# Four small edits to a fused attention and mixture-of-experts kernel: ones multiplied at the start, the sort's first step moved, the first gate later, the last bias earlier

## The chip, the core and the metric

The kernel runs on one core of a Trainium2 chip. The time is the device's, in microseconds (us), from launch to end; lower is better. The engines are TensorE (PE in the profile), VectorE (DVE), ScalarE (ACT), GpSimd (POOL) and SyncE, which here issues most transfers (SP). Each takes its instructions in its own order and waits for the others through semaphores.

## The reference

The input is `x`, 64 sequences of 64 tokens with 256 features, and one type (0, 1 or 2) for each sequence. Everything is fp32. Two blocks follow each other, each with a residual:

```python
x = x + attention(cond(x, type))
x = x + moe(cond2(x, type))
```

- `cond`: a gated FFN (`gelu(x @ wi0) * (x @ wi1) @ wo`, 256 to 1024 to 256) with the weights of the sequence's type, and one with shared weights. A gate mixes the two: a softmax over two logits, from the first token of each sequence, `softmax(relu(concat(expert[:, 0], share[:, 0]) @ g0) @ g1)`.
- `attention`: causal, 16 heads of 16, within each sequence, with biases.
- `cond2`: two typed experts and three shared FFNs, mixed by a gate in the same manner.
- `moe`: a router of three layers, the two best of eight experts for each token, at most 10 tokens per sequence and expert, and for each expert `relu(x @ W1 + b1) @ W2 + b2`, scaled by the router's weight and added up.

## The kernel before, in words

The sequences are sorted by type, so that most groups share weights. The sort runs on the chip: `sort()` is a Python generator which yields between its steps, so that a few small operations at a time can be put between others. Its first step (lines 577 and 579) turns the types into 64 x 3 flags on DVE; two empty steps later a pair of small products with a matrix of ones counts each type and ranks each sequence (tile `p`). The ones are filled by POOL in `masks()` (line 501).

Sequences are handled in eight superblocks of eight (512 tokens). A layer multiplies with Strassen's scheme: seven products p1 to p7 of half-size blocks, whose sums are made on DVE, ACT and POOL. In the up products (`strassen`) each product needs a PSUM bank of a pool of four, until DVE or ACT has read it; p3 is added into the bank of p5, and so must wait until DVE has taken p5 out of it (line 256). The down products go into accumulating banks of their own, `sa...` (p1, p6, p2, p7) and `sb...` (p5, p3, p4). `layer` gives each superblock items of a `first` (up) and a `second` (down) half, and `pipeline` runs the `first` of the next item before the `second` of this one.

At the start, `load_x(0)` fetches the tokens of superblock 0 in two halves, eight pieces of the shared weights follow on the same queue, and the types come by ACT's queue (line 444). `turn_x(0)` transposes the tokens on TensorE into two banks (tile `px`), of which ACT copies the first and DVE the second (line 835). `tc.issue_after` holds DVE's copy behind the last cast of the counters (`K.cast`). Then come the sums for the products, on DVE and POOL, and the Strassen products of the shared layer (names ending in `c`).

Side work is slipped in through a list, `between`: each call of `tick` takes one entry, and where an entry is flagged as needing room, ticks that offer none pass it by. An entry of `None` is an empty step. The sort is trickled in this way (15 entries), and in the typed layers (names ending in `e`) so are the gate and the attention of an earlier superblock: `begin_cond(s)` appends the gate's steps and then `attention(s)`. It is called after the `first` of one item and before the `second` of the one before it. The gate's steps are

- `hidden`: products of the typed tokens (`tw1`) and the shared part with `g0` (tile `pha`), copied by ACT (line 1248),
- `add_up`, `logits`, `spread`: small products (`pfa`, `plga`, `pgwa`) with a softmax between them,
- `sums`: the weighted sum on DVE, after which `fetch1` of the next superblock issues its eight fetches on SP.

`m2`, `m3` and `whole` are the last attention steps of the superblock before; for superblock 0 they are empty. In a typed superblock there are 12 ticks in each of two `first` halves and 3 in the `second` of item 0, after p1/p6, p2/p7 and p5/p3. `tw1` is filled by `fetch_typed`: the typed result is written to DRAM (`spillt`) and read back in sorted order, in eight transfers, each with an address read from a table.

In the last stage, `down` multiplies the hidden values of an expert with its second weights for five tiles of 128 slots (`po`). For each tile DVE adds the bias, ACT scales by the router's weight, and POOL scatters the rows with an add into the output. For the very last tile the bias is scaled first, by ACT (line 2023), so that one DVE operation (line 2024) does the rest. This scaled bias lies in one of the four slots that the results go round in: the one of tile 1.

Which instruction stands where on its engine is settled when the program is built: the framework's scheduler goes by the order of the code and by what it reckons to be ready, so that neighbours can change places (p4 runs ahead of p3 in the first superblock).

## Time and profile before

| | us |
|---|---|
| median of the runs | 2747.27 |
| the three runs | 2747.27, 2744.07, 2747.38 |
| the profiled execution, its own time | 2744.14 |
| its span (first to last instruction) | 2742.5 |
| busy in it: TensorE | 2709.1 |
| busy in it: VectorE | 1626.9 |
| busy in it: GpSimd | 1065.2 |
| busy in it: ScalarE | 837.1 |

The profile is of one execution; its times are counted from its first instruction. A row of the timeline gives the start, the length, the engine, the line, the operation, the tile written and read, the shape and the number of instructions; brackets at its end hold the time for which the engine had been idle, and what ended that. Most matmuls are recorded by a helper on line 119, so they are told apart by their tiles. An fp32 product stands as two records, a transpose as one. The lengths of matmuls overlap their successors, so starts are what counts. In the table by windows, the columns of an engine are its busy time and its number of instructions, and behind them comes the granted TensorE clock, as a share of the full one. In the span's first 12.84 us the clock isn't recorded and the table gives 1.00.

### The profile page before, as it was taken

To read this page: it belongs to the slowest core of one execution; us is meant where nothing else is said; L and a number is where in the kernel's file an instruction comes from. 1 tells how busy PE (TensorE), PEld (TensorE's weight loads), DVE (VectorE), ACT (ScalarE), POOL (GpSimd) and SP (SyncE) were. 2 spreads that over 40 slices of the span, in tenths; PEclk is the share of its full clock that TensorE was granted. 3 is DMA by queue.
4 is the path that set the end of the run, shared out by engine and by line. 5 is a ranking of instruction groups with operands and counts; after the bars stand their busy time and mean duration, and the time that the engine had idled before them with its cause. 6 is when DMAs were issued, how large, how long until landed. Compare 5 with 4: busy or idle time off the path is not lost.

```text
span 2742.5 us, 38338 instructions
## 1 busy us (share of the span) xinstructions
PE 2709.1 (99%) x13765; PEld 2232.6 (81%) x13765; DVE 1626.9 (59%) x2931; ACT 837.1 (31%) x1535; POOL 1065.2 (39%) x1121
## 2 busy tenths in 40 slices
PE   8999999999999999999999999999999999999998
PEld 7888887677767778888888888888888888877777
DVE  7887467888887774535546766667443333332443
ACT  2221124544444332212222222222222222322333
POOL 4555123343335667634323332325323322324332
PEclk9999999999999999999999999999999999999999
DMA  4554545343342123652443434444200000013330
GB/s 118 159 173 141 191 149 185 97 128 128 104 147 88 63 101 135 207 183 81 154 136 126 150 132 146 147 139 135 70 17 6 9 5 6 5 52 79 96 92 2
DMA packets 236365, 293.47 MB, mean 107 GB/s; under 512 B 141624, under 2 KB 199824, under 8 KB 236048
## 3 DMA queue, kind: packets, MB, share of 16 engines
q1 hardware_dynamic: 214608, 231.44, 26.9%
q0 software_dynamic: 21344, 58.54, 6.3%
q8 instruction: 109, 1.79, 0.3%
q10 hardware_dynamic: 224, 1.05, 0.1%
q14 instruction: 80, 0.66, 0.1%
HBM read 208.80 MB, written 83.99 MB: 107 GB/s over the span
## 4 chain that ended last, share of the span: by engine, by line
PE 91%; DVE 4%; issue 2%; DMA 2%; ACT 0%; SPq 0%; POOL 0%; POOLq 0%; DVEq 0%; ACTq 0%
PE sad L119 6%; PE p5r L119 5%; PE p1r L119 5%; PE po L119 5%; PE sbd L119 4%; PE sat L119 4%; PE p5d L119 3%; PE p1d L119 3%; PE sbt L119 3%; PE p6r L119 2%; PE p4r L119 2%; PE p7r L119 2%; PE p5e L119 2%; PE p1e L119 2%; PE p5t L119 2%; PE sac L119 2%
## 5 line engine op out<-in xcount | busy, mean ns | idle before, releaser
L198 POOL TENSOR_TENSOR arena<-arena 128x512 f32<-128x512 f32 (+1 forms) x175 | 236.3, 1350 | 667.2 <-DVE arena L195 659.3
L199 POOL TENSOR_TENSOR arena<-arena 128x512 f32<-128x512 f32 (+1 forms) x175 | 213.5, 1220 | 18.0 <-DVE arena L196 17.0
L119 PE MATMUL sad<-arena 128*128 128x256 f32 x768 | 176.7, 380 | 0.0
L119 PE MATMUL po<-arena 128*128 128x256 f32 (+1 forms) x704 | 169.8, 399 | 0.1
L119 PEld LDWEIGHTS sad<-arena 128*128 128x128 f32 x768 | 144.0, 190 | 19.6 <-issue 0.8
L119 PEld LDWEIGHTS po<-arena 128*128 128x128 f32 x704 | 132.9, 190 | 28.4 <-issue 11.0
L119 PE MATMUL p5r<-arena 128*128 128x256 f32 x640 | 149.7, 381 | 0.5 <-DVE arena L256 0.5
L119 PE MATMUL p1r<-arena 128*128 128x256 f32 x640 | 150.0, 382 | 0.0
L195 POOL TENSOR_TENSOR arena<-arena 128x256 f32<-128x256 f32 (+1 forms) x55 | 45.1, 821 | 260.8 <-ACT arena L1740 80.7
L1902 POOL DMA_INDIRECT xs<-arena,slot_i x64 | 62.6, 978 | 199.9 <-ACT arena L1898 108.7
L119 PEld LDWEIGHTS p1r<-arena 128*128 128x128 f32 x640 | 120.0, 190 | 21.2 <-issue 5.9
L119 PEld LDWEIGHTS p5r<-arena 128*128 128x128 f32 x640 | 120.8, 190 | 17.6 <-DVE arena L256 1.4
L119 PE MATMUL sbd<-arena 128*128 128x256 f32 x576 | 134.8, 381 | 0.0
L195 DVE TENSOR_TENSOR arena<-arena 128x512 f32<-128x512 f32 (+2 forms) x127 | 96.8, 762 | 63.2 <-ACT arena L332 34.2
L119 PEld LDWEIGHTS sbd<-arena 128*128 128x128 f32 x576 | 108.5, 190 | 17.5 <-POOL arena L199 2.2
L188 POOL TENSOR_TENSOR arena<-arena 128x256 f32<-128x256 f32 (+1 forms) x53 | 47.9, 905 | 184.8 <-DMA arena<-in_L_cond_share_wo 43.3
L119 PE MATMUL sat<-arena 128*128 128x256 f32 x512 | 118.6, 382 | 0.8 <-POOL arena L198 0.8
L196 DVE TENSOR_TENSOR arena<-arena 128x512 f32<-128x512 f32 (+2 forms) x127 | 108.8, 856 | 3.5
L2028 POOL DMA_INDIRECT out<-arena,rows_i x40 | 61.9, 1547 | 123.4 <-ACT arena L2027 66.9
L119 PEld LDWEIGHTS sat<-arena 128*128 128x128 f32 x512 | 96.2, 190 | 14.0 <-POOL arena L198 1.2
L332 ACT ACTIVATE arena<-arena 128x512 f32<-128x512 f32 x144 | 90.3, 628 | 45.6 <-DVE arena L267 21.6
L119 PE MATMUL p5d<-arena 128*128 128x256 f32 x384 | 99.7, 382 | 2.4 <-DVE arena L256 2.4
(452 smaller groups left out, 6243.5 us busy)
## 6 DMA issues: line engine op xcount, KB each, us to landing
arena<-sums_i SPq DMA_DIRECT2D x32, 896.0 KB
arena<-sums_2i SPq DMA_DIRECT2D x32, 896.0 KB
arena<-sums_2o SPq DMA_DIRECT2D x32, 896.0 KB
arena<-in_L_ffn_eW SPq DMA_DIRECT2D x16, 1024.0 KB
arena<-sums_o SPq DMA_DIRECT2D x16, 896.0 KB
spill<-arena SPq DMA_DIRECT2D x24, 512.0 KB
arena<-spill POOLq DMA_DIRECT2D x24, 512.0 KB, 6.1
sums_i<-arena POOLq DMA_DIRECT2D x12, 896.0 KB, 3.9
```

The costliest lines, as they stand in the source:

```text
L119: nc.tensor.matmul(o, lhsT=lhsT, rhs=rhs, start=start, stop=stop, skip_group_check=shared_bank)
L188: eng.tensor_add(s1, a21, a22)
L195: eng.tensor_sub(t1, b12, b11)
L196: r = eng.tensor_sub(t2, b22, t1)
L198: eng2.tensor_sub(t3, b22, b12)
L199: return r.ins, eng2.tensor_sub(t4, b21, t2).ins
L332: nc.scalar.activation(c_out(ij), src, AF.Relu)
L1902: nc.gpsimd.indirect_dma_start(out=to.rearrange("e n w -> (e n) w"), out_offset=bass.IndirectOffsetOnAxis(ap=slot_i[:, n, i : i + 1], axis=0),
L2028: nc.gpsimd.indirect_dma_start(out=out_rows, out_offset=bass.IndirectOffsetOnAxis(ap=row_i[:, u : u + 1], axis=0), in_=eo, in_offset=None, ...
```

## The change

It has four parts.

1. The matrix of ones is filled by DVE near the top, and TensorE multiplies it with itself six times into a bank `idle` that nothing reads. POOL's fill of it is gone.
2. The first step of the sort (the two DVE operations) is issued ahead of the tokens' transposes, and `K.cast`, behind which DVE's copy of the tokens stands, now is its second operation. A `yield` more keeps the later steps at the same entries of the list.
3. For superblock 0, two empty entries are put ahead of the gate's first step.
4. In the last expert, the scaled bias is made before the first tile's products, into a slot of its own.

```diff
@@ setup
     ident = const.tile([P, P], F32, name="ident")
     make_identity(nc, ident)
+    K.ones = const.tile([P, P], F32, name="ones")
+    nc.vector.memset(K.ones, 1.0)
+
+    idle = bank("idle")
+    for _ in range(6):
+        mm(idle[:, 0:P], K.ones, K.ones)
     up1 = [weight_blocks(t, AT_S + 14 * j + 8) for j, t in enumerate(swi)]
...
     def masks():
-        K.ones = const.tile([P, P], F32, name="ones")
-        nc.gpsimd.memset(K.ones, 1.0)
...
@@ sort
         oh = tmp([NB, NTYPE], "oh")
-        nc.vector.tensor_scalar(oh, iota18[0:NB, 0:NTYPE], typ, None, ALU.is_equal)
+        K.cast = nc.vector.tensor_scalar(oh, iota18[0:NB, 0:NTYPE], typ, None, ALU.is_equal)
+        yield
         yield
         yield
         p0 = bank("p0")
...
     masks()
     counters()
+    next(sorting)
 
     with tc.issue_after(K.cast.ins):
         turned = turn_x(0)
...
@@ begin_cond
         m2, m3, whole = rest[0]
-        between.extend(hidden + m2 + add_up + logits + m3 + no * 2 + spread + no + sums + whole + no)
+        between.extend((no * 2 if s == 0 else []) + hidden + m2 + add_up + logits + m3 + no * 2 + spread + no + sums + whole + no)
         between.extend(attention(s))
...
@@ down
         row_i = rows_i[:, e]
+        if e == E - 1:
+            bw = area(AT_EO + 4, D)
+            nc.scalar.activation(bw, b2[:, e, :], AF.Copy, scale=xr[:, NU - 1, D + 1 : D + 2])
         for u in us:
...
             by = xr[:, u, D + 1 : D + 2]
             if e == E - 1 and u == NU - 1:
 
-                bw = area(AT_EO + (e * NU + u + 1) % 4, D)
-                nc.scalar.activation(bw, b2[:, e, :], AF.Copy, scale=by)
                 nc.vector.scalar_tensor_tensor(eo, po, by, bw, ALU.mult, ALU.add)
```

## The prediction

> **What bounds the kernel now.** I read the page first. TensorE has work nearly all the time, so only the microseconds in which it stands still or runs slowly can be won.

> ```profile
> PE 2709.1 (99%) x13765; PEld 2232.6 (81%) x13765; DVE 1626.9 (59%) x2931; ACT 837.1 (31%) x1535; POOL 1065.2 (39%) x1121
> ```

> The view of waits for TensorE then lists whom it waited for (total, times, longest, in us). The rows that touch the change:

> ```profile
> PE px L831 <- POOL arena L480: 3.9, 1, 3.9
> ...
> PE pha L119 <- DMA arena<-spillt: 2.3, 1, 2.3
> PE ppT L1419 <- ACT arena L1248: 2.1, 5, 0.4
> ...
> PE p L119 <- DVE arena L579: 1.7, 1, 1.7
> ```

> The reader is to see four places: the start until tokens arrive, the first gate's product `pha`, which waits for a transfer, a small wait of every later superblock beside the gate's copy (L1248), and the sort's first product `p`. Together 10.0 us, 0.36% of the span. [...]

> The table by windows (length, PE busy, records, then the granted clock) tells what the first gate's wait costs beyond itself:

> ```profile
> 12.85:16.30 3.45, 1.76 (x9) 1.21 (x8) 3.40 (x7) 0.51 (x1) 3.37 (x6) 1.00 1.06 335
> ...
> 412.20:415.60 3.40, 1.07 (x11) 0.38 (x10) 2.46 (x3) 0.00 (x0) 2.04 (x2) 1.00 0.42 83
> 415.60:419.00 3.40, 3.40 (x9) 2.69 (x10) 0.00 (x0) 0.37 (x1) 1.49 (x2) 0.50 1.01 420
> 419.00:422.40 3.40, 3.40 (x19) 3.07 (x18) 0.17 (x1) 0.00 (x0) 0.00 (x0) 1.00 0.99 402
> ```

> After the window with 1.07 us of work the clock was halved for one window; 1.76 us of work in a window left it whole. So half speed begins somewhere between 31% and 51% of busy time. The timeline of TensorE shows the price (start, us, records):

> ```profile
> 410.66 1.89 PE L119 MATMUL sae<-arena 128*128 128x256 f32 x8
> 414.87 0.67 PE L119 MATMUL pha<-arena 128*32 128x256 f32 x8 [2.33 <-DMA arena<-spillt]
> 415.47 2.83 PE L119 MATMUL sae<-arena 128*128 128x256 f32 x6
> 418.09 2.36 PE L119 MATMUL sbe<-arena 128*128 128x256 f32 x8
> ...
> 443.98 1.46 PE L119 MATMUL sae<-arena 128*128 128x256 f32 x6
> 445.28 2.75 PE L119 MATMUL sbe<-arena 128*128 128x256 f32 x12
> ```

> From start to next start, six `sae` records take 2.62 us after the wait and 1.30 us one layer later.

> **The change, part by part.**

> *Gate two steps later.* [...] Before, the first superblock's `hidden` is taken at the first tick of the down products, after p1 and p6, and stood in TensorE's order behind ten `sae` records. Two empty entries put it on the third tick, behind the other six `sae` (1.30 us) and eight `sbe` (eight twelfths of 2.59, 1.73 us). The next record could start at 412.4, so `hidden` comes up at 415.4; its tokens were there at 414.87. The margin is only 0.5 us (1.0 if two records slip ahead again). Gain: the wait, 2.33 us, and the half clock, (2.62 - 1.30) for six `sae` and (2.19 - 1.73) for eight `sbe`, 1.78 us. Sum 4.1 us.

> [...] The trace has the half clock behind 2.33 us, so I take 4.1 for this execution. [...]

> What moves with it: the steps `hidden` to `sums` of superblock 0 issue nine products (18 records), a copy and an exponential on ACT, eight short and six long DVE operations, nothing on POOL, and then eight fetches on the SP queue (from 436.66, 10.05 us). Behind these on SP stand the ring's weights (446.95) and the typed tokens' round trip (448.85 to 466.4). Two ticks in the up products are 1.7 us; the next gate needs the tokens at 480.8, so about 14 us hide it.

> *All later gates move too.* A typed superblock has 27 ticks and its list 26 entries, and ticks that an entry with a room flag refuses add to that: counted through the code, one entry was left over at each later begin, and with the change three are, up to superblock 6; only at the end of typed stage 7 are ticks forced, four instead of two. So `hidden` of superblocks 1 to 6 leaves the down products and falls into the next up products, with `mix(2)` 0.86 us behind it instead of about 1.7, while the Strassen products hold banks too. The windows table of one superblock has 67.06 us busy of 68.00, and the gaps are 0.2 before `sc`, 0.43 before `ppT`, 0.34 before `ov`. These become others. I see no sign; bounds: all of it gone, 6 x 1.0 = 6 us faster, or doubled, 6 us slower; nearest row is the superblock's own 0.94 us, so I take 0, with 2 us either way as likely.

> *Sort's first step ahead of the copy.* Two small DVE operations, 0.13 and 0.78 us (L577, L579), leave 14.55 and 15.34 for the gap between the casts (done 5.31) and the second token copy at 6.55; their input's last packet landed at 3.87. If 0.78 were again its length they end at 6.2, still before 6.55. The rows at the old place:

> ```profile
> 14.55 0.13 DVE L577 TENSOR_SCALAR arena<-typ_i 64x1 f32<-64x1 int32 x1
> 15.34 0.78 DVE L579 TENSOR_SCALAR arena<-arena 64x3 f32<-64x3 f32 x1
> 16.04 0.67 DVE L256 TENSOR_TENSOR arena<-p5c,arena 128x512 f32<-128x512 f32 x1
> 16.27 0.35 PE L119 MATMUL p<-arena,ones 64*128 64x3 f32 x2 [1.69 <-DVE arena L579]
> 17.72 1.03 PE L119 MATMUL p5c<-arena 128*128 128x256 f32 x4
> ```

> TensorE was free from 14.58. With the flags ready, `p` (0.5 us) and p4 (0.97) run there, until about 16.0. What is late next is L256, which must read p5 before p3 goes into the same bank: without the two operations DVE reaches it 0.7 us sooner, done at 16.0. p3 starts at 16.0 instead of 17.72. Gain 1.7 us; I take 1.5, since DVE is full from 21 to 33 us and may give some back. [...]

> *Ones.* The fill goes from POOL (0.20 us) to DVE, idle until 3.07; about 0.2 there, hidden. Six products of 128 columns are twelve records. A record of 256 columns in the half-clock stretch takes 0.437 us; half, 0.22 (an estimate), makes 2.6 us, from about 1.1 to 3.7. The tokens' first transpose is at 3.93: hidden, and if the cover is gone (TensorE begins at 1.9, say) 0.5 us late. Do they raise the clock? The window 6.00 to 9.40 held 2.83 us of records, transposes among them, and the products behind it were still slow (p6 2.04 us for four against 1.03), so 83% wasn't enough. [...] Even a warm clock by 8 us would then wait for DVE's L256 at 16.0. I take 0; bounds +0.5 and -0.6.

> *Bias.* In the last layer ACT's scaled bias waits for a slot that the scatter of tile 1 reads:

> ```profile
> 2728.80 0.51 ACT L2023 ACTIVATE arena<-arena 128x256 f32<-128x256 f32 x1 [3.06 <-DMA out<-arena,rows_i]
> 2729.21 0.49 ACT L2027 ACTIVATE arena<-arena 128x256 f32<-128x256 f32 x1
> 2729.98 1.54 POOL L2028 DMA_INDIRECT out<-arena,rows_i  x1 [2.40 <-ACT arena L2027]
> 2733.43 1.54 POOL L2028 DMA_INDIRECT out<-arena,rows_i  x1 [1.91 <-DMA out<-arena,rows_i]
> 2736.92 1.54 POOL L2028 DMA_INDIRECT out<-arena,rows_i  x1 [1.95 <-DMA out<-arena,rows_i]
> ```

> It stands ahead of tile 2's scaling; the scatters then follow each other at 3.45 us, each waiting for the one before. Made into a slot of its own before the first product (ACT idles there for 2.4 us), tile 2's scatter starts at about 2729.47, when tile 1's (2726.04 + 3.4) lands. The two behind shift alike: 0.5 us. Between 0 and 0.55.

> **Sum.** 4.1 + 1.5 + 0 + 0 + 0.5 = 6.1 us off the profiled execution's 2744.14: 2738.0. The median of the runs shown is 2747.27, 3.1 above it; what those lost I can't see (a later clock grant at the start, a longer wait for the fetched tokens). I carry half of that: 2739.6.

> **Rivals.**
> - *All four act, later gates neutral* (0.57): 2739.6, between 2736 and 2742.5.
> - *The transfer or the clock gives less* (0.20): the gap crossed a window boundary in the usual run, or the fetch lands 1 us later and `hidden` still waits; only 2.3 or less is won, or p3 stays tied to a slow p5 (start gain 0.3). For it: the margin of 0.5 us. Then 2747.3 - 2.3 - 0.3 - 0.5 is about 2744.
> - *Later gates give it back* (0.13): six superblocks with 0.6 to 1 us more, 2744 to 2747; nothing measurable.
> - *Slower* (0.10): one mechanism, in superblocks 1 to 6: `mix(2)`'s transposes want two banks while the up products hold theirs, and the gap grows until a window has under half its time busy. It decides from 1.7 us of idleness in one 3.4 us window; then a superblock pays that, less the 0.4 it pays now, and the half clock, 1.7 us: 3.0 x 6 = 18, so 2739.6 + 18 = 2757.6. Against it: gaps there are 0.43 at most now, and the scheduler moves products into them.
> - That an edit does nothing can be for the ones alone; it is in the sum at 0.

> **How the numbers follow.** A difference of 0.2% (5.5 us, about what a measurement of this kernel can tell from no change) puts the line at 2741.8. The first case lies under it nine times in ten, the second and third a fifth of the time at most: 0.51 + 0.04, and 0.05 for later gates that lose their gaps: 0.60. Slower 0.10, same 0.30. The range leaves out the slower case and the last parts of gain: 2735.5 to 2746.5.

> **What would show it.** `pha` with no wait for `spillt` and no half clock at 415; `p` without its 1.7 us wait and p3 near 16.0; the last three scatters 0.5 us sooner against the last product; the sum of waits between 480 and 1010 us within 2 us of now. Wrong if `pha` still waits, if superblocks 1 to 6 take over 68.5 us each, or if the half clock appears elsewhere.

## The result, and the profile after

The changed kernel takes 2785.47 us in the median of four runs (2785.16 to 2788.46), the kernel before 2746.97 in the same comparison (2744.07 to 2747.38). The ratio is 1.0147, with a 95% interval from 1.0136 to 1.0159: slower by about 39 us, where 7.7 us less had been predicted. The profiled execution took 2785.35 us, its span is 2783.6 us.

The table of engines of the kernel after (busy time, share of the span, instructions):

```profile
PE 2713.8 (97%) x13777; PEld 2232.2 (80%) x13777; DVE 1628.1 (58%) x2932; ACT 845.1 (30%) x1543; POOL 1072.2 (39%) x1120
```

TensorE's busy time rose by 4.7 us, the span by 41.1. So some 36 us of the loss are idle time that TensorE did not have before. No engine has much more work. The one count that the diff doesn't explain is ACT's: eight instructions more.

The starts of the gate's product `pha`, one for each typed superblock, tell where the time goes:

| superblock | 0 | 1 | 2 | 3 | 4 | 5 | 6 | 7 |
|---|---|---|---|---|---|---|---|---|
| before, us | 414.87 | 480.82 | 547.63 | 615.69 | 683.70 | 751.73 | 820.93 | 898.13 |
| after, us | 417.47 | 483.13 | 557.14 | 634.45 | 707.90 | 788.47 | 864.17 | 940.31 |

From superblock 1 to 6 it is 340.1 us before and 381.0 after: 8 us more on average for each of five periods (5.4 to 12.5). At a down product behind the last of these gates (a block of tile `sad`, 938.3 before, 981.4 after) the distance is 43.1 us, at the last product of the kernel 41.6. Two microseconds of it are there when the typed stage begins; nearly all of the rest arises in that stage.

The view of waits of TensorE of the kernel after (total, times, longest, in us) shows what it waits for there:

```profile
PE ov L119 <- issue: 12.7, 5, 2.5
PE p6e L119 <- ACT arena L1372: 10.3, 4, 2.6
PE pha L119 <- ACT arena L1372: 7.8, 1, 7.8
PE p6e L119 <- DVE arena L1452: 3.7, 5, 0.7
...
PE ppT L1424 <- DVE arena L1401: 3.1, 3, 1.2
...
PE p6d L119 <- ACT arena L1372: 2.6, 1, 2.6
...
PE p1e L119 <- DMA arena<-sums_i: 0.9, 1, 0.9
```

The rows that the prediction started from are gone: `px` waits 0.2 us, `p` not at all, `pha` no longer for `spillt` and `ppT` no longer for the gate's copy. In their place stand waits behind one copy of ACT, L1372, of 20.7 us together, and 12.7 us of `ov`, the attention's product with the values. In all rows but the last, a product of the attention waits, or one that waits for the attention, though the edit only names the gate.

Two chains of the timeline (start, length, engine, line, operation, tiles, shape; in brackets the idle time before and its releaser) show how such a wait comes about. First the values of the attention, around 474 to 482 us of the kernel after:

```profile
474.33 1.78 POOL L198 TENSOR_TENSOR arena<-arena 128x512 f32<-128x512 f32 x1 [5.08 <-DVE arena L195]
476.08 1.27 POOL L199 TENSOR_TENSOR arena<-arena 128x512 f32<-128x512 f32 x1
477.31 1.24 POOL L1375 TENSOR_TENSOR arena<-arena,vrest 128x256 f32<-128x256 f32 x1
...
480.76 0.72 POOL L1379 TENSOR_TENSOR arena<-arena,vmask 64x256 f32<-64x256 f32 x1
481.51 0.37 ACT L1372 COPY arena<-pv 128x256 f32<-128x256 f32 x1 [6.33 <-POOL arena L1379]
...
481.93 1.27 PE L119 MATMUL p6e<-arena 128*128 128x256 f32 x4 [2.57 <-ACT arena L1372]
```

An attention step `values(i)` makes a product `pv`, ACT copies it out of its bank into the slot `vn` (L1372), and POOL spreads it from there (L1375, L1379). There is one slot. POOL has two sums of tokens (L198, L199) in its queue ahead of the spreading of `values(2)`, so this ends at 481.48. Until then ACT's copy of `values(3)` can't write the slot, the product stays in its PSUM bank, and `p6e` waits 2.57 us for that copy: it needs the bank, as the code has it.

The kernel before at the same place (its lines 1367 and 1370 are 1372 and 1375 after):

```profile
472.58 0.37 ACT L1367 COPY arena<-pv 128x256 f32<-128x256 f32 x1 [2.21 <-POOL arena L195]
...
474.35 1.27 POOL L1370 TENSOR_TENSOR arena<-arena,vrest 128x256 f32<-128x256 f32 x1
...
480.22 0.37 ACT L1367 COPY arena<-pv 128x256 f32<-128x256 f32 x1
480.43 1.66 POOL L198 TENSOR_TENSOR arena<-arena 128x512 f32<-128x512 f32 x1 [0.69 <-DVE arena L195]
```

There the spreading of `values(2)` comes first on POOL, and the 128x512 sums start only when the copy of `values(3)` has begun.

The second chain is on ACT, at 495 to 501 us of the kernel after:

```profile
495.44 0.66 PE L1424 MATMUL ppT<-ident,arena 128*128 128x128 f32 x4
...
496.31 1.28 ACT L1278 ACT_TABLE_LOAD   x1
...
497.61 0.20 ACT L1278 ACTIVATE gwa<-gwa 8x2 f32<-8x2 f32 x1
497.83 1.28 ACT L320 ACT_TABLE_LOAD   x1
...
499.12 0.63 ACT L320 ACTIVATE arena<-arena 128x512 f32<-128x512 f32 x1
499.66 1.05 ACT L1429 COPY arena<-ppT 128x512 f32<-128x512 f32 x2
...
500.81 0.67 PE L119 MATMUL ov<-arena 128*32 128x64 f32 x32 [2.55 <-issue]
```

The gate's exponential (0.20 us) now falls between two of the FFN's activations (L320). ACT loads a table for it and another one back, 1.28 us each; the copy of the last attention step's transposes (L1429) stands in ACT's order behind all this, and `ov` needs that copy. The kernel before in the same superblock (L1273, L1424 are L1278, L1429 after):

```profile
490.65 1.28 ACT L1273 ACT_TABLE_LOAD   x1
...
492.70 0.20 ACT L1273 ACTIVATE gwa<-gwa 8x2 f32<-8x2 f32 x1 [0.77 <-DVE gwa L1272]
...
493.83 1.07 ACT L1424 COPY arena<-ppT 128x512 f32<-128x512 f32 x2 [0.93 <-PE ppT L1419]
...
495.00 0.82 PE L119 MATMUL ov<-arena 128*32 128x64 f32 x32 [0.39 <-issue]
...
496.52 1.28 ACT L320 ACT_TABLE_LOAD   x1
```

Here both loads are there too, but the copy comes ahead of the second one, and `ov` waits 0.39 us. In superblocks 2 to 5 the kernel before loads nothing for the gate's exponential: there it stands directly behind two of the attention's own exponentials (L1403), at 557.65, 625.70, 693.72 and 761.75 us, and takes 0.19 us. So ACT's eight additional instructions are loads: 6 of them at L1278 and 24 at L320, where before there were 2 and 20.

The table by windows of the kernel after (window, length, PE busy with records, PEld, DVE, ACT, POOL, granted clock, DMA share, GB/s) shows what the waits bring with them:

```profile
479.40:482.80 3.40, 0.87 (x4) 0.68 (x4) 0.66 (x2) 1.29 (x3) 2.85 (x6) 1.00 0.19 43
482.80:486.20 3.40, 3.40 (x15) 1.80 (x14) 3.40 (x7) 2.26 (x4) 2.30 (x4) 0.50 0.18 39
634.40:707.90 73.50, 67.30 (x451) 46.96 (x451) 56.65 (x105) 35.57 (x59) 23.31 (x28) 0.99 0.33 105
707.90:788.50 80.60, 68.61 (x457) 48.00 (x456) 63.49 (x117) 36.60 (x60) 26.71 (x33) 0.95 0.33 106
```

Behind a window with 0.87 us of products comes one at half clock; there are six such places between 480 and 812 us, where before, past the start, only the one at 415.6 stood. The two last rows are a period each of 73.50 and 80.60 us. Before, both were 68.0 with 67.0 busy. In the second of them the chain with the one slot is at its worst:

```profile
788.47 1.09 PE L119 MATMUL pha<-arena 128*32 128x256 f32 x8 [7.84 <-ACT arena L1372]
```

### The profile page after: what moved, and what is told of

It reads as the page before. It is cut to its first block, busy times and chain, and to the rows that moved or that the text cites. A ratio compares the mean times of both kernels' runs of the same rounds, so it can differ in the third digit from the quotient of the medians.

```text
span 2783.6 us, 38369 instructions
## 1 busy us (share of the span) xinstructions
PE 2713.8 (97%) x13777; PEld 2232.2 (80%) x13777; DVE 1628.1 (58%) x2932; ACT 845.1 (30%) x1543; POOL 1072.2 (39%) x1120
## 4 chain that ended last, share of the span: by engine, by line
PE 83%; DVE 9%; issue 3%; DMA 2%; POOL 2%; ACT 1%; SPq 0%; POOLq 0%; DVEq 0%; ACTq 0%
PE sad L119 5%; PE p1r L119 5%; PE p5r L119 5%; PE po L119 5%; PE sbd L119 4%; PE sat L119 4%; PE p5d L119 3%; PE sbt L119 3%; PE p1d L119 3%; PE p6r L119 2%; PE p4r L119 2%; PE p7r L119 2%; PE p5t L119 2%; PE p1t L119 2%; PE p5e L119 2%
## 5 line engine op out<-in xcount | busy, mean ns | idle before, releaser
L198 POOL TENSOR_TENSOR arena<-arena 128x512 f32<-128x512 f32 (+1 forms) x175 | 241.5, 1380 | 707.6 <-DVE arena L195 701.4
L199 POOL TENSOR_TENSOR arena<-arena 128x512 f32<-128x512 f32 (+1 forms) x175 | 211.3, 1208 | 8.6 <-DVE arena L196 8.4
L119 PE MATMUL sad<-arena 128*128 128x256 f32 x768 | 176.5, 380 | 0.0
L119 PE MATMUL po<-arena 128*128 128x256 f32 (+1 forms) x704 | 170.6, 399 | 0.1
L119 PEld LDWEIGHTS sad<-arena 128*128 128x128 f32 x768 | 144.1, 190 | 19.5 <-issue 0.8
L119 PEld LDWEIGHTS po<-arena 128*128 128x128 f32 x704 | 133.0, 190 | 26.2 <-issue 8.6
L119 PE MATMUL p5r<-arena 128*128 128x256 f32 x640 | 149.6, 381 | 0.5 <-DVE arena L256 0.5
L119 PE MATMUL p1r<-arena 128*128 128x256 f32 x640 | 150.1, 382 | 0.0
L119 PEld LDWEIGHTS p1r<-arena 128*128 128x128 f32 x640 | 120.1, 190 | 21.1 <-issue 5.9
L119 PEld LDWEIGHTS p5r<-arena 128*128 128x128 f32 x640 | 121.0, 190 | 17.3 <-DVE arena L256 1.1
L119 PE MATMUL sbd<-arena 128*128 128x256 f32 x576 | 134.8, 381 | 0.0
L119 PEld LDWEIGHTS sbd<-arena 128*128 128x128 f32 x576 | 108.6, 190 | 17.5 <-POOL arena L199 2.3
L119 PE MATMUL sat<-arena 128*128 128x256 f32 x512 | 118.6, 382 | 0.6 <-POOL arena L198 0.6
L119 PEld LDWEIGHTS sat<-arena 128*128 128x128 f32 x512 | 96.2, 190 | 13.7 <-POOL arena L198 1.0
L119 PE MATMUL p5d<-arena 128*128 128x256 f32 x384 | 99.4, 382 | 3.2 <-DVE arena L256 3.2
```

The lines of the kernel that those rows point to most:

```text
L119: nc.tensor.matmul(o, lhsT=lhsT, rhs=rhs, start=start, stop=stop, skip_group_check=shared_bank)
L198: eng2.tensor_sub(t3, b22, b12)
L199: return r.ins, eng2.tensor_sub(t4, b21, t2).ins
```

## The experiments

Each kernel ran beside runs of the kernel before on the same chip; medians, ratios and intervals are against these. Medians of the kernel before were 2745.5 to 2746.8 in the three comparisons. The ratios are the record's, and can differ from the quotient of the medians by up to 0.07%.

**Which part costs it.** First the change without its third part, then the third part alone, and then all four parts with the first superblock's gate moved while later ones stay where they were (below, "the first gate alone moved"). For the last, the empty steps m2 and m3 of superblock 0 are left out to make up for the two that are added, so that the length of the list stays the same.

```diff
 change without part 3 (against after)
-        between.extend((no * 2 if s == 0 else []) + hidden + m2 + ...
+        between.extend(hidden + m2 + ...
```

> The changed kernel without its third part (the two empty entries); ones, sort step and bias stay. Theory A (the two entries are never made up for, so that the attention steps of superblocks 1 to 6 stand two ticks later, at places where they stall TensorE): all of the 40 us go, the time is 2744 to 2747 (start 1.7 us and end 0.5 us won, 3.7 us lost again in the shared layer, which the trace shows already). Theory B (the earlier start shifts everything against GpSimd and the transfers, and the losses of the typed layers come from there): about 2785.

2746.46 us against 2745.51, ratio 1.0004 (0.9994 to 1.0013): no difference.

```diff
 part 3 alone (against before)
-        between.extend(hidden + m2 + ...
+        between.extend((no * 2 if s == 0 else []) + hidden + m2 + ...
```

> The kernel before with the third part alone. Theory A: 2785 to 2789, the same waits of 2.5 us before p6e and ov in superblocks 1 to 6, and half clocks there. Theory B: 2743, that is the first gate's 4.1 us less than before and nothing else.

2786.58 us, ratio 1.0152 (1.0137 to 1.0168). The third part does all of it; the other three together make nothing that can be measured, where the prediction had 2.0 us for them.

```diff
 the first gate alone is moved (against after)
+        if s == 0:
+            between.extend(no * 2 + hidden + add_up + logits + no * 2 + spread + no + sums + whole + no)
+        else:
+            between.extend(hidden + m2 + add_up + logits + m3 + no * 2 + spread + no + sums + whole + no)
```

> The changed kernel, but the two empty entries ahead of the first gate are taken out again from its own list (the two empty places of m2 and m3, which superblock 0 does not need), so that everything from its weighted sum on stands at the old ticks. Theory A: no wait for the fetched tokens, no half clock near 415 us, superblocks of 68.0 us as before: 4.1 us below the kernel without the third part, about 2741. Theory B: 2780 or more. Rival C (the later place of the gate's own product is what costs): slower than the kernel without the third part.

2743.11 us, ratio 0.9994 (0.9985 to 1.0002). `pha` of superblocks 1 and 6 starts at 478.8 and 817.9 here, five periods of 67.8 us (68.0 before), although the first gate is as late as in the change. So it isn't the first gate's own place that costs, but that the steps of all later superblocks move too. The fetches on SP, which follow `sums`, keep their old ticks in this kernel; that their later place in the change doesn't cost is read from its view of waits, where no product waits for a transfer from the second superblock to the end of the typed stage.

**How much is a step worth.** One empty entry in place of two:

```diff
-        between.extend((no * 2 if s == 0 else []) + hidden + m2 + ...
+        between.extend((no if s == 0 else []) + hidden + m2 + ...
```

> The changed kernel with one empty entry ahead of the first gate instead of two. By the count of ticks, one entry is made up for within superblock 0 (a tick that a step without room had refused is no longer lost), so one entry is left at each later begin, as before; two are not made up for. Theory A: the later superblocks are as before (68.0 us each), the first gate still waits about 1 us for its tokens, the time is 2742 to 2746. Rival: each entry costs about the same, half of the 41 us: 2765.

2746.62 us, ratio 1.0005 (0.9994 to 1.0015). The period is 68.0 us (479.95 to 820.19 for five), and `pha` still waits 0.7 us for `spillt`. By the count of ticks, the first entry is made up for within superblock 0 and the second isn't; the times agree: there is an edge between one and two, and no slope.

**What the moved steps wait for.** To take away the wait for the slot, a second one:

```diff
-            vn = area(AT_VN, D)
+            vn = area((AT_VN, 171)[i % 2], D)
```

> The changed kernel in full, with two slots instead of one for the copy of the values (vn). Theory A1 (the copy of values(3) waits for GpSimd to finish with values(2), and holds a PSUM bank that p6 needs): the waits on that copy go, five of 2.6 us and one of 7.8 us, and the half clocks that follow them: 20 us or more off, 2755 to 2765; the waits of 2.5 us before ov stay. Theory A2 (the bank or ACT's order is at fault, not the slot): no change, 2783 to 2787.

2767.23 us against 2745.51, ratio 1.0084 (1.0069 to 1.0100). In its view of waits the rows with L1372 that the kernel after had for `p6e`, `pha` and `p6d` are gone, those of `ov` and of `p6e` behind DVE stay as they were, and `ppT` waits longer:

```profile
PE ov L119 <- issue: 12.7, 5, 2.5
PE ppT L1424 <- DVE arena L1401: 7.0, 7, 1.2
...
PE p6e L119 <- DVE arena L1452: 3.7, 5, 0.7
```

The place of the first chain, without the wait:

```profile
474.12 0.37 ACT L1372 COPY arena<-pv 128x256 f32<-128x256 f32 x1 [1.33 <-PE pv L119]
...
476.81 1.03 PE L119 MATMUL p6e<-arena 128*128 128x256 f32 x4
```

The five periods fell from 381.0 to 359.5 us in the profile. That execution took 2758.82 us, the shortest of the four, at a mean clock of 1.000. The other three took 7.3 to 10.2 us longer and ran at 0.995 to 0.997; where their clock was lower this profile doesn't show. In it, the clock stayed whole behind the five waits of `ov`, the longest 2.5 us.

Then, on top of this, the exponential of this gate alone is taken off ACT. DVE computes 1 + x in its place, so that there is no table to load:

```diff
-            nc.scalar.activation(w, w, AF.Exp)
+            if name[0] == "a":
+                nc.vector.tensor_scalar(w, w, 1.0, None, ALU.add)
+            else:
+                nc.scalar.activation(w, w, AF.Exp)
```

> The changed kernel with two slots for the copy of the values, and with the first block's gate softmax taken as 1 + x on VectorE instead of exp on ScalarE (this leaves out the true exponential, so ScalarE needs no other table for it). Theory A (the five waits of 2.55 us before ov come from ScalarE: the gate's exp and its two table loads of 1.28 us stand ahead of the copies of mix(3)'s transposes): those waits shrink to under 0.8 us and the time falls by 8 to 13 us against two slots alone (2767), to 2754 to 2759. Theory B (ov waits for something else, DVE or the products' order): no change, 2764 to 2769.

2751.83 us against 2745.63, ratio 1.0021 (1.0012 to 1.0030). Its timeline at the place of the second chain, and its waits (lines 1427 and 1432 here are 1424 and 1429 after):

```profile
495.99 0.63 ACT L320 ACTIVATE arena<-arena 128x512 f32<-128x512 f32 x1 [1.43 <-DVE arena L261]
496.53 1.05 ACT L1432 COPY arena<-ppT 128x512 f32<-128x512 f32 x2
...
497.68 0.67 PE L119 MATMUL ov<-arena 128*32 128x64 f32 x32 [1.15 <-issue]
```

```profile
PE ppT L1427 <- DVE arena L1404: 6.7, 7, 1.2
PE ov L119 <- issue: 5.8, 5, 1.2
...
PE p6e L119 <- DVE arena L1455: 3.7, 5, 0.7
```

The copy of the transposes follows the FFN's activation at once, and `ov` waits 1.15 us instead of 2.55. So against their own runs of before the distance went from 38.5 us to 21.7 with two slots, and to 6.2 without the exponential as well: about 17 us hang on the slot, about 15 on the exponential with its table loads, in this order; the exponential was not taken away while there was one slot. The waits of `ov` that went are only 6.9 us of the 15. The rest fits the granted clock: the one execution with two slots that had the whole clock, 2758.82 us, is 7.0 above the median of this kernel (mean clock 0.998 to 1.000), and the other three, 14.3 to 17.2 above it, are those with the lower clock (0.995 to 0.997). Where it was lower no profile shows. Of what is left, the five periods of this kernel still take 350.4 us, 10.3 more than before, about what the rows behind DVE above hold (`ppT` 6.7, `p6e` 3.7); that they are the cause is argued, and what makes DVE late there wasn't tried.

**What the first gate wins where nothing else moves.** With the first gate alone moved, `pha` doesn't wait, and the half clock at 415 us is gone (1.00 granted from 414.0 to 420.8 us, 0.74 and 0.76 in the two halves of it in the kernel before), which the prediction put at 4.1 us. The kernel to set beside it is the change without part 3, 2746.46 us in the same comparison: it is 3.4 us faster (an estimate by resampling the twelve times of each: 1.1 to 5.3). The timeline of TensorE of that kernel, and its window:

```profile
415.73 0.67 PE L119 MATMUL pha<-arena 128*32 128x256 f32 x8
...
418.92 1.10 PE L119 MATMUL p1e<-arena 128*128 128x256 f32 x4 [1.46 <-DMA arena<-sums_i]
```

```profile
417.40:420.80 3.40, 1.94 (x11) 1.70 (x10) 0.00 (x0) 0.59 (x1) 0.00 (x0) 1.00 1.02 416
```

The next up product now waits 1.46 us for its weights, of which the transfer engines are full at that time (DMA share 1.02, 416 GB/s). Part of the wait has been passed on from one transfer to the next. To take it away, one weight load was hung one item later:

```diff
-        hook(more[3 + 5 * i], lambda v=halves2[3 - i]: sum_half(*v, AT_SUM2))
+        hook(more[3 + 5 * i + (i == 1)], lambda v=halves2[3 - i]: sum_half(*v, AT_SUM2))
```

> The kernel whose two empty entries are taken out again from the first gate's own list, and in which the load of one half of a shared weight (0.5 MB twice, beside the ring's weights at 416 us) is issued one item later. Theory A (with the gate's wait gone, the next layer's weights are late, because the transfer engines are full from 415 to 419 us): the wait of 1.5 us at p1e goes, 1 to 1.5 us less than with that load in place. Rival: p1e waits as long, its weights are late for their own issue time; no change.

2750.94 us, ratio 1.0017 (1.0008 to 1.0025): worse. The view of waits begins with a new row:

```profile
PE sc L119 <- ACT arena L1372: 4.4, 1, 4.4
```

It stands at 462 us, and half speed follows it: the four records of `p5e` from 465.04 us take 1.92 us, those from 454.87 took 1.03. It is the slot `vn` again: the delayed sums of the weights stand on POOL ahead of the spreading of the values before, and keep the next copy back. That a later load brings a gain is not upheld; `p1e` still waits 0.83 us for its weights.

**The start.** Each of the first two parts alone (one time each, so the landmarks of their profiles are read, not their times):

```diff
 part 1 alone (against before)
+    K.ones = const.tile([P, P], F32, name="ones")
+    nc.vector.memset(K.ones, 1.0)
+    idle = bank("idle")
+    for _ in range(6):
+        mm(idle[:, 0:P], K.ones, K.ones)
...
-        K.ones = const.tile([P, P], F32, name="ones")
-        nc.gpsimd.memset(K.ones, 1.0)
```

> The kernel before with the first part alone (ones filled by VectorE and multiplied six times). Theory A: the clock is granted before 8 us, where the kernel before had it at 12.8, and the first down products (sac, at 39.4 us before) start no more than 0.3 us sooner, because DVE's sort step still holds the product p until 15 to 16 us. Rival: the warm start alone brings the 1.7 us.

One time, 2749.27 us. The clock was granted at 13.7 us, and the first shared down product (tile `sac`) starts at 38.57 us, 39.45 before.

```diff
 part 2 alone (against before)
-        nc.vector.tensor_scalar(oh, iota18[0:NB, 0:NTYPE], typ, None, ALU.is_equal)
+        K.cast = nc.vector.tensor_scalar(oh, iota18[0:NB, 0:NTYPE], typ, None, ALU.is_equal)
+        yield
...
     counters()
+    next(sorting)
```

> The kernel before with the second part alone (the sort's first step ahead of the tokens' copy). From the sum: the product p no longer waits 1.7 us for DVE, and the first down products (sac, 39.4 us before) start 1.0 to 1.7 us sooner, 37.7 to 38.4, though the clock is granted no sooner than in the kernel before. Rival: without the warm start TensorE's slow products take the place of the wait, under 0.5 us sooner.

One time, 2742.95 us. `sac` starts at 38.43, the wait of `p` is gone, and at the first typed down product (tile `sae`) this kernel is still 1.2 us ahead of before (357.76 against 358.93). The same landmark is at 360.89 in the kernel after, 2.0 us behind before, though its `sac` at 37.72 was 1.7 us ahead. So what the start gains is lost again within the shared layers. But the gain itself is no more than executions differ: with part 3 alone, which leaves the start as it was, `sac` starts at 38.50, and in the last kernel below, whose start is that of before too, at 41.89.

In the kernel after, TensorE waits 4.7 us for DVE between 42 and 361 us, before 1.4; that is most of the 3.7 us lost there. One such place is larger in the kernel with the first gate alone moved, timeline of DVE, POOL and TensorE at 103 to 108 us:

```profile
103.15 1.28 POOL L198 TENSOR_TENSOR arena<-arena 128x512 f32<-128x512 f32 x1
103.61 2.76 DVE L672 TENSOR_TENSOR arena<-arena 128x3 f32<-128x3 f32 x1
104.39 1.27 POOL L199 TENSOR_TENSOR arena<-arena 128x512 f32<-128x512 f32 x1
105.61 0.72 POOL L188 TENSOR_TENSOR arena<-arena 128x256 f32<-128x256 f32 x1
106.28 0.68 DVE L251 TENSOR_TENSOR arena<-p7c,arena 128x512 f32<-128x512 f32 x1
...
107.81 0.92 PE L119 MATMUL p5c<-arena 128*128 128x256 f32 x3 [2.06 <-DVE arena L256]
```

An addition of three columns takes 2.76 us and ends with the third of the POOL sums beside it; DVE's reading of the banks comes late, and `p5c` waits 2.06 us. (In the kernel after the same addition takes 0.59 us, before 0.98.) To take it away this one addition goes to POOL:

```diff
 on top of the first gate alone moved
-        nc.vector.tensor_add(end, first, cnt)
+        nc.gpsimd.tensor_add(end, first, cnt)
```

> All four parts, the gate's two entries taken out again from its own list, and the first step of the unit table (an addition of 128 x 3, line 672) on GpSimd instead of VectorE. Theory D (that VectorE operation, 2.76 us long instead of 0.15 because it stands beside GpSimd's two sums, holds up the reading of p7 and p5, and so the products): the wait of 2.06 us at p5c near 108 us goes, and 2 us or more are won, 2740 to 2742. Rival (VectorE would be late there anyway, or the next step stands as long): the wait stays above 1 us and nothing is won.

The addition takes 0.19 us there, the wait of `p5c` is gone, and the next superblock's first `sac` starts at 112.59 instead of 114.84. But the time is 2743.26 us, ratio 0.9989 (0.9979 to 0.9999), where the kernel without this edit had 2743.11 in the first comparison (0.9994): longer waits, up to 2.0 us, come between 120 and 235 us, and at 361.58 `sae` is behind before. The place was found, a gain was not.

The first gate and the bias, without the parts at the start:

```diff
 against before: the first gate alone moved, as above, and part 4
+        if e == E - 1:
+            bw = area(AT_EO + 4, D)
+            nc.scalar.activation(bw, b2[:, e, :], AF.Copy, scale=xr[:, NU - 1, D + 1 : D + 2])
...
-                bw = area(AT_EO + (e * NU + u + 1) % 4, D)
-                nc.scalar.activation(bw, b2[:, e, :], AF.Copy, scale=by)
```

> The kernel before with the fourth part (bias) and with the first gate two ticks later inside its own list only; no ones, sort step at its old place. Theory D (the start's 1.7 us are given back in the shared layer, where a short VectorE step stands still beside GpSimd from 103 to 107 us and TensorE waits 2 us for it, so parts 1 and 2 are worth nothing): as fast as the same kernel with parts 1 and 2 or faster, 2741 to 2744, with no wait over 1 us near 108 us. Rival: the start's 1.7 us stay, and this kernel is 1.7 us slower than the one with all parts, 2744.8 or more.

2743.73 us, ratio 0.9996 (0.9984 to 1.0008). Its profile has the start at its worst (`p` waits 3.07 us, half speed from 15.1 to 22.0, `sac` at 41.89) and a wait of 2.31 us at 111.9. That no such wait would be there without the moved sort was wrong.

No version is ahead of the kernel before by a margin worth having. The nearest are those with the first gate alone moved, at 0.9989 to 0.9996; of their intervals only that of the one with the addition on POOL (0.9979 to 0.9999) lies below 1.

## Why the prediction was wrong, point by point

- **Later gates: the step that failed.** The prediction counted the list rightly, three entries left over instead of one, and saw that the steps of superblocks 1 to 6 move. It priced this at 0, with 2 us either way as likely and 6 as the bound, because the superblock's own gaps came to 0.94 us. That is the room in the old order; it says nothing on what a new order waits for. The loss was about 8 us for each of five periods, 41 us in all. Only `hidden` and `mix(2)` were followed to their new places. The steps ahead of these in the list, `values(2)`, `mix(1)` and `values(3)`, move too, so that the sums of tokens come ahead of the spreading of the values in POOL's order, where they had stood behind it.
- **The slower rival** had the place (superblocks 1 to 6), the kind (a bank that is kept while products want one) and the half clock that follows. That it came true is in part luck: it gave `mix(2)`'s transposes as the cause and 3.0 us for each superblock. In the runs the slot of the values was worth about 17 us and the exponential with its tables about 15. Its chance of 0.10 rested on gaps of 0.43 us at most, the same mistake. That the scheduler moves products into gaps was no help, since the products themselves wanted the bank.
- **What ACT does in between** isn't in the prediction. It listed "a copy and an exponential on ACT" and took them for short ones; 0.20 us is what the exponential takes, but with both loads it is 2.8 us, from 496.31 to 499.11. The loads were in the trace of before (490.65 and 496.52); what stands behind them on ACT was not asked.
- **First gate, 4.1 us.** Right in its mechanism: two steps later `pha` waits for nothing and the clock stays whole (1.00 granted from 414.0 to 420.8 us in the kernel after). Of the gain, about 3.4 us are left in the time, and 0.8 to 1.5 us went into the next layer's wait for its weights, which the prediction had looked at only on SP's queue behind the gate, and not on the full transfer engines at 417 to 421 us (DMA share 1.02). That the gap can cross a boundary between two windows, the case of the second rival, no run shows: in the profile of before it lies within one, from 412.21 to 415.61 us.
- **Sort's first step, 1.5 us.** Right at its place: with this part alone the wait of `p` is gone and p3 starts at 15.99, where the prediction had 16.0. `sac` came 1.0 us sooner, 1.7 with the ones, in one execution each. But the gain was carried to the end of the sum as if nothing lay between, and in the kernel after new waits for DVE spent it before 361 us.
- **Ones, 0.** Right in the time, wrong in the reason. In this execution the clock was whole from 4.9 us (12.8 before), and L256, which was to hold p3 until 16.0, came at 13.43.

```profile
1.50:4.90 3.40, 3.21 (x15) 2.62 (x14) 0.82 (x9) 1.20 (x1) 2.68 (x18) 1.00 0.71 197
```

This window has 3.21 us of records, ones and transposes together. With the ones alone the clock came at 13.7 us, later than before, so in these runs the ones do not settle when it comes. No run shows the bound of 0.6 us as time won; what this execution shows in its place is that the last six transposes (`px`) took 0.89 us, 1.54 before. In this execution p3 starts at 14.27 (17.72 before); of these 3.4 us, 1.7 are left at `sac`, and 1.3 went in waits for DVE between 20 and 30 us, where the kernel before lost 0.3. That the products behind would wait for DVE was foreseen, only at a later place than the prediction had it.
- **Bias, 0.5 us.** Right. The scaled bias no longer waits for the slot, and from the first of the last layer's five scatters to the last it is 13.93 us, 14.36 before: 0.43 us won. The last three scatters of the kernel after:

```profile
2771.14 1.55 POOL L2035 DMA_INDIRECT out<-arena,rows_i  x1 [1.93 <-ACT arena L2034]
2774.60 1.55 POOL L2035 DMA_INDIRECT out<-arena,rows_i  x1 [1.92 <-ACT arena L2034]
2778.10 1.55 POOL L2035 DMA_INDIRECT out<-arena,rows_i  x1 [1.95 <-DMA out<-arena,rows_i]
```

Only the last of them still waits for the scatter ahead of it; before, the last two did, and the first came late because the bias did.
- **What would show it** held up: superblocks above 68.5 us and half clock elsewhere were named as the signs of being wrong, and both are there. Its first sign, `pha` without a wait and no half clock at 415, is there as well.

## What to carry to other kernels

Where side steps are dealt out one to a tick, an edit that adds an entry moves every later step: follow each of them to its new tick and ask, for its slots, its banks and each of its queues, what stands ahead of it there. The idle time of the old order is no measure of the new one; two entries cost 39 us here and one cost nothing. To delay one step, delay it at the expense of empty entries further on, so that the rest of the list stays in its place; done so, the first gate's move won about 3 us of its 4.
